# Summing each group's four edge tiles in one burst, and building one-hot matrices two groups ahead

## The chip, the core and the metric

The kernel runs on one core of a Trainium2 chip. The core has five engines with an instruction queue each: TensorE (PE in the profile; PEld is its weight load), VectorE (DVE), ScalarE (ACT), GpSimd (POOL) and SyncE (SP). Each takes its own queue in order and waits on semaphores for the others. The metric is the device time of one execution in microseconds; before the change its median was 3282.5 us over 3 runs.

## The reference

The input is a graph of 6250 nodes with 512 features each (f32) and 100,000 edges, sorted by their target. The output is

```python
x = x + gnn(layernorm(x), src, dst)      # two layers
x = x + moe(layernorm(x))                # 8 experts, the best 2 of each node
# one layer of gnn:
agg = segment_sum(h[src], dst)           # sum of the source rows of a node's edges
h = relu(h @ W_self + (agg / max(deg, 1)) @ W_neigh + b)
# moe, per expert: relu(x @ W1 + b1) @ W2 + b2, layernorm with gamma and beta,
# weighted by the softmax of the two best logits x @ Wg
```

## The kernel before

**Tiles.** The edges are cut into 782 tiles of 128. Three consecutive tiles make a chunk; its targets lie within 32 nodes from the chunk's first. Four chunks fill the 128 partitions of one PSUM tile `pa`, 32 partitions (a strip) each. The sum over edges is a matmul: a one-hot matrix of 128 edges x 32 nodes (`hot`) is the stationary operand, the 128 gathered source rows of 512 features are the moving one. A matmul in f32 is two instructions in the profile.

**Slots.** The loop `sums` (L194) runs over slots `i`. A slot is the four tiles, one of each chunk, with the same place in their chunks; three slots close a group of twelve tiles. There are 196 slots in a layer (the last has two tiles), and 49 blocks of 128 output nodes, about one per four slots. For each slot:

- `gather(i + ahead)` (L210) issues four indirect DMAs on GpSimd's queue (L214), each of 128 rows of 2 KB. They land in a ring: 16 buffers in stage 1 (`rows_t`, three slots ahead), 12 in stage 2 (parts of `big`, two ahead). A gather waits until the matmul that read its buffer last is done.
- `build(i + 1)` (L218) makes the next slot's one-hot matrices on VectorE (L224), in one of four buffers. In stage 1 it also adds the slots of a group up for the counts of edges (L234, `few`).
- `add` (L237) runs the four matmuls (L244), each on its own 32 columns of the array. The slot's work named "mid" stands between the second and the third of them.
- `close` (L247), at the end of a group, copies `pa` to a strip in SBUF on ScalarE (L252), and in stage 1 counts by a matmul (L256) and a copy (L259).
- The work named "post" comes last. `take_out` (L272) is one of it: it picks a block's 128 nodes from the strips by matmuls with `sel` (L278; L280 for the counts), made by `prepare` (L269).

**Stage 1** (`layer1`, L379) does the first GNN layer and the projections for the second. `take_out` starts a chain for each block: `u0` (post, one slot later) projects the block's own rows (L386). `u1` (mid, two later) transposes the aggregate (L188, four transpositions, copied from PSUM by ScalarE, L190), and `u2` (post, same slot) projects the copy (L386). `u3` (mid, three later) and `u4` (post, same slot) do the same with the result, `u5` follows a slot later.

**Stage 2** (`route`, L761) does the second aggregation, routes each node and fills experts' work in. Its chain is `turn` (mid, 2; L188 and L190), `logits` (post, 2; L775 and a copy L777), `experts` (mid, 3; L781, then VectorE), `rank` (mid, 4; L793, L794, then VectorE), two `send`s (mid, 5 and 6; an indirect DMA on GpSimd, L823), `turn_gates` (post, 5; L809) and `share` (post, 6; L816, L817). From about slot 77 on, every second slot starts an expert's tile: `turn_x` (mid; L188 and L190), `times` (post, same slot; L709, copied by L712) and `turn_h` (post, next slot; L717, L720).

The order on TensorE, VectorE, ScalarE and GpSimd is that of the program's text here (a manual schedule). Stage 3, after it, runs the rest of the experts and combines. `apart` (L533) writes one element on GpSimd (L535); before, only the sends of the last four blocks have it ahead of them.

Of the kernel before, what the change touches and what calls it, by code (L numbers as in the profile page):

```python
# [40 lines left out]
SW = 32  # L41
NQ = P // SW
TS = 3
# [24 lines left out]
def gnn_moe(ctx, tc, x, src, dst, Ws1, Wn1, gb1, Ws2, Wn2, gb2, Wg, W1, b1, W2, b2, gamma, beta, out):  # L68
    nc = tc.nc
# [7 lines left out]
    NB = (N + P - 1) // P  # L77
    rows = [min(P, N - b * P) for b in range(NB)]
    NT_E = (E + P - 1) // P
# [114 lines left out]
    def sums(z, pool, pap, room, pn, finish, ring, nring, each=None):  # L194

        nslot = (NG - 1) * TS + min(TS, NT_E - (NG - 1) * NQ * TS)  # L200
        ahead = nring // NQ - 1
        tiles = [[t for t in range(i // TS * NQ * TS + i % TS, min(NT_E, (i // TS + 1) * NQ * TS), TS)]
                 for i in range(nslot)]
        gathered, hots, few, strips, counts, sels, due = {}, {}, {}, {}, {}, {}, {}
        pa = [None]

        def at(i, place, what):
            due.setdefault((i, place), []).append(what)

        def gather(i):  # L210
            if i < nslot:
                for t in tiles[i]:
                    gathered[t] = ring()
                    nc.gpsimd.indirect_dma_start(  # L214
                        out=gathered[t], out_offset=None, in_=z[:, :],
                        in_offset=bass.IndirectOffsetOnAxis(ap=srcT[:, t : t + 1], axis=0))

        def build(i):  # L218
            if i >= nslot:
                return  # L220
            g, j = divmod(i, TS)
            m = len(tiles[i])
            hots[i] = pool.tile([P, NQ, SW], F32, name="hot", bufs=4)
            nc.vector.tensor_tensor(  # L224
                hots[i][:, :m],
                rel.rearrange("p (c j) -> p j c", j=TS)[:, j, g * NQ : g * NQ + m]
                .rearrange("p (t o) -> p t o", o=1).to_broadcast([P, m, SW]),
                iota_row[:, :SW].rearrange("p (o m) -> p o m", o=1).to_broadcast([P, m, SW]), OP.is_equal)
            if pn is not None and j:

                end = j == TS - 1 or i == nslot - 1
                few[g] = pool.tile([P, NQ, SW], BF16 if end else F32, name=f"few{int(end)}", bufs=1)
                before = hots[i - 1] if j == 1 else few[g, 1]
                nc.vector.tensor_add(few[g][:, :m], before[:, :m], hots[i][:, :m])  # L234
                few[g, j] = few[g]

        def add(i, qs):  # L237
            g, j = divmod(i, TS)
            if pa[0] is None:
                pa[0] = pap.tile([P, D], F32, name="pa", bufs=2)  # L240
            for q in qs:
                if q < len(tiles[i]):
                    t = tiles[i][q]
                    nc.tensor.matmul(pa[0][q * SW : (q + 1) * SW], hots[i][:, q], gathered.pop(t), start=(j == 0),  # L244
                                     stop=(j == TS - 1 or t == NT_E - 1), tile_position=(0, q * SW))

        def close(i):  # L247

            g = i // TS
            k = len(tiles[i]) * SW  # L250
            st = pool.tile([P, D], F32, name="st_", bufs=most)
            nc.scalar.copy(st[:k], pa[0][:k])  # L252
            strips[g] = st, k
            pa[0] = None
            if pn is not None:
                nc.tensor.matmul(pn[:k, 0], few[g].rearrange("p q m -> p (q m)")[:, :k], ones_h[:, :NDEG],  # L256
                                 start=True, stop=True)
                counts[g] = pool.tile([P, NDEG], F32, name="counts", bufs=most + 1)
                nc.vector.tensor_copy(counts[g][:k], pn[:k, 0])  # L259
            for b in range(NB):  # L260
                if reach[b][1] == g:
                    at(i + 1, "mid", lambda b=b: prepare(b))
                    at(i + 1, "post", lambda b=b: take_out(i + 1, b))

        def prepare(b):
            for g in range(reach[b][0], reach[b][1] + 1):
                k = strips[g][1]
                sels[b, g] = pool.tile([P, P], F32, name="sel", bufs=most)
                nc.vector.tensor_scalar(sels[b, g][:k], iota_row[:k], float(b * P), node[:k, g : g + 1],  # L269
                                        op0=OP.add, op1=OP.is_equal)  # L270

        def take_out(i, b):  # L272
            a, z = reach[b]
            ps = room()
            for g in range(a, z + 1):
                st, k = strips[g]
                sel = sels.pop((b, g))
                nc.tensor.matmul(ps, sel[:k], st[:k], start=(g == a), stop=(g == z))  # L278
                if pn is not None:
                    nc.tensor.matmul(pn[:, 1], sel[:k], counts[g][:k], start=(g == a), stop=(g == z))  # L280
            for behind, place, what in finish(b, ps) if pn is None else finish(b, ps, pn[:, 1]):
                at(i + behind, place, what)

        for i in range(ahead):
            gather(i)
        build(0)
        i = 0
        while i < nslot or any(k[0] >= i for k in due):
            gather(i + ahead)
            if each is not None:  # L290
                for behind, place, what in each(i):
                    at(i + behind, place, what)
            build(i + 1)
            if i < nslot:
                add(i, (0, 1))
            for what in due.pop((i, "mid"), ()):
                what()
            if i < nslot:
                add(i, (2, 3))
                if i % TS == TS - 1 or i == nslot - 1:  # L300
                    close(i)
            for what in due.pop((i, "post"), ()):
                what()
            i += 1
# [31 lines left out]
    with tc.tile_pool(name="l0", bufs=3, side="right") as pool, \  # L336
# [15 lines left out]
        for i, (b0, m) in enumerate(batch):  # L352
# [5 lines left out]
            for t in range(m):  # L358
                mv, rs = norm_stats(pool, xt[:n, t], n)
                nc.vector.tensor_scalar(xn[:n, t], xt[:n, t], mv[:n, 0:1], rs[:n], op0=OP.subtract, op1=OP.mult)  # L360
                b = b0 + t
# [13 lines left out]
    with tc.tile_pool(name="s1", bufs=2, side="right") as pool, \  # L375
# [55 lines left out]
        with tc.manual_schedule(engines=HAND):  # L431
            sums(xn_d, pool, pap, lambda: pap.tile([P, D], F32, name="ps"),
                 pap.tile([P, 2, NDEG], F32, name="pn"), layer1,
                 lambda: pool.tile([P, D], F32, name="rows_t", bufs=16), 16)
# [91 lines left out]
    def free_of(inst, group, keep=()):  # L526

        tc.declare_no_dep(inst.ins, group=group, reason="distinct rows", keep=keep)
        tc.add_to_no_dep_group(group, inst.ins)
# [3 lines left out]
    def apart():  # L533

        nc.gpsimd.memset(tick, 0.0)  # L535
# [200 lines left out]
    with tc.tile_pool(name="s2", bufs=2, side="right") as pool, \  # L736
# [11 lines left out]
        def ring():  # L748
            nring[0] += 1
            return part(NW + (nring[0] - 1) % 12)  # L750
# [10 lines left out]
        def route(b, pa):  # L761
# [4 lines left out]
            t = {}  # L766
# [51 lines left out]
                nc.sync.dma_start(accs[r], acc[:n])  # L818

            def send(k):  # L820
                if b >= NB - 4:
                    apart()
                inst = nc.gpsimd.indirect_dma_start(  # L823
                    out=xs[:, :], out_offset=bass.IndirectOffsetOnAxis(ap=slot[:n, b, k : k + 1], axis=0),
                    in_=t["xn"][:n], in_offset=None)
                free_of(inst, "xs")
# [20 lines left out]
        def each(i):  # L847

            at_slot[0] = i
            j = up_next[0]  # L850
            if i % 2 or j >= upto_n[-1]:
                return []
            c = max(c for c in range(len(n0)) if n0[c] <= j)
            if ready.get(c, 1 << 30) > i:
                return []
            up_next[0] += 1
            u = Up(j, pool, psp)
            u.fetch()
            return [(3, "mid", u.turn_x), (3, "post", u.times), (4, "post", u.turn_h)]

        fetch_own(0)
        with tc.manual_schedule(engines=HAND):
            sums(z2, pool, pap, lambda: psp.tile([P, D], F32, name="ph"), None, route, ring, 12, each)
# [4 lines left out]
    with tc.tile_pool(name="io", bufs=2, side="right") as io, \  # L868
# [114 lines left out]
        def finish(i, e, py, mv, rs):  # L983
            nc.vector.reciprocal(rs, rs)
            y = io.tile([P, D], F32, name="y")
            nc.vector.scalar_tensor_tensor(y, py, mv[:, 0:1], gmb[:, bass.ds(e * D, D)],  # L986
                                           op0=OP.subtract, op1=OP.mult)
            nc.scalar.activation(y, y, AF.Copy, scale=rs)
            nc.sync.dma_start(ys[i * P : (i + 1) * P, :], y)
# [208 lines left out]
```

## Time and profile before

| what | us |
|---|---|
| median of 3 runs (3280.7 to 3284.3) | 3282.5 |
| the profiled execution | 3665.7 |
| its span, first to last instruction | 3663.9 |
| mean granted TensorE clock in it | 0.903 |
| stage 1 (150 to 1440 us of the span) | 1290 |
| stage 2 (1508 to 2920) | 1412 |
| stage 3 (2920 to the end) | 744 |

The page of the profile gives each engine's busy time, then the span in 40 slices (a digit is the busy share in tenths; PEclk is the granted clock), the chain of work that ended last, and groups of equal instructions. Other views are used too: busy time in stretches (windows), the waits (who waited for whom: microseconds, times, longest), and the timeline. In a timeline, `[0.30 <-PE pa L244]` is idle time of the engine ahead of the instruction and what ended it; "issue" is time in which it waited for nothing that the profile shows.

### The profile page before, as it was taken

The page shows a single profiled execution, that of the slowest core. Times are in us where ns is not written, and L with a number is a line of the kernel's source. Part 1 is how long each engine was busy: PE and PEld are TensorE (multiplying, and loading weights), DVE is VectorE, ACT ScalarE, POOL GpSimd, SP SyncE. Part 2 cuts the span into 40 slices and gives each one's busy share as a digit, 9 for nine tenths or more (in the row PEclk, how much of TensorE's full clock was granted, in tenths as well). Part 3 has the DMA queues.
Part 4 walks back from the last instruction along what each step waited for, and adds up shares of the span by engine and source line. Part 5 has one row for each costly group of instructions (what it writes and reads, how often), then busy time and mean ns, then how long its engine had stood idle before and what let it go on. Part 6 is the DMA issues. An engine that isn't in the chain of part 4 may idle for free.

```text
span 3663.9 us, 33902 instructions
## 1 busy us (share of the span) xinstructions
PE 3038.6 (83%) x9794; PEld 1156.2 (32%) x9794; DVE 1131.4 (31%) x4001; ACT 659.3 (18%) x1188; POOL 1800.4 (49%) x1970
## 2 busy tenths in 40 slices
PE   7778888999999999466666888888888877999994
PEld 3223333333333333111111333333333333334442
DVE  5311111111111111132233333433343334443464
ACT  1211111111111111011111222222222211222221
POOL 0266555555555552466666555555555438000253
PEclk9889999999999999777777888898898988999997
DMA  6566666665666653666666766666677634441496
GB/s 241 183 186 203 199 195 200 192 185 177 185 188 176 178 171 103 239 200 208 199 204 200 214 214 215 209 217 213 214 228 218 189 105 155 135 132 61 156 308 233
DMA packets 269498, 698.76 MB, mean 191 GB/s; under 512 B 42448, under 2 KB 44090, under 8 KB 269148
## 3 DMA queue, kind: packets, MB, share of 16 engines
q0 software_dynamic: 142912, 463.42, 42.9%
q1 hardware_dynamic: 121372, 224.59, 17.9%
q10 hardware_dynamic: 5024, 8.50, 0.7%
q8 instruction: 85, 1.39, 0.2%
q14 instruction: 105, 0.86, 0.1%
HBM read 557.43 MB, written 139.71 MB: 190 GB/s over the span
## 4 chain that ended last, share of the span: by engine, by line
PE 70%; another core or an unknown queue 10%; DVE 7%; issue 6%; DMA 4%; ACT 2%; SPq 0%; DVEq 0%; POOL 0%; ACTq 0%; POOLq 0%
PE pm L386 17%; PE pa L244 15%; PE py L969 9%; PE ph L709 7%; PE ph L278 5%; PE pt L188 4%; PE ph L945 3%; PE ps L278 2%; PE ph L816 2%; PE pm L366 2%; DMA out<-acc 1%; PE small L775 1%; DMA xt<-in_x 1%; PE pt L717 1%
## 5 line engine op out<-in xcount | busy, mean ns | idle before, releaser
L214 POOL DMA_INDIRECT rows_t<-xn_d,srcT x782 | 742.1, 949 | 654.9 <-PE pa L244 262.9
L214 POOL DMA_INDIRECT big<-z,srcT x782 | 752.6, 962 | 609.3 <-issue 167.9
L244 PE MATMUL pa<-big,hot 128*32 128x512 f32 x1564 | 443.9, 684 | 107.5 <-DVE hot L224 63.0
L969 PE MATMUL py<-w,hT 128*128 x840 | 395.4, 614 | 40.4 <-DVE y L986 21.8
L244 PE MATMUL pa<-rows_t,hot 128*32 128x512 f32 x1564 | 348.5, 632 | 93.1 <-DVE hot L224 30.0
L386 PE MATMUL pm<-wn,tT 128*128 128x512 f32 x784 | 368.6, 613 | 22.0 <-ACT tT L190 21.7
L709 PE MATMUL ph<-big,xgT 128*128 x544 | 288.7, 680 | 68.7 <-ACT xgT L190 24.0
L905 POOL DMA_INDIRECT big<-ys,yrow x98 | 107.4, 1096 | 427.6 <-DMA ys<-y 331.3
L969 PEld LDWEIGHTS py<-w,hT 128*128 128x128 f32 x840 | 153.6, 193 | 219.3 <-issue 172.1
L386 PEld LDWEIGHTS pm<-wn,tT 128*128 128x128 f32 x784 | 144.9, 195 | 207.8 <-issue 163.7
L709 PEld LDWEIGHTS ph<-big,xgT 128*128 128x128 f32 x544 | 113.2, 219 | 230.5 <-issue 143.9
L386 PE MATMUL pm<-ws,tT 128*128 128x512 f32 x392 | 181.1, 605 | 0.0
L190 ACT ACTIVATE tT<-pt 128x512 f32<-128x512 f32 x117 | 69.0, 596 | 565.4 <-PE pt L188 408.7
L244 PEld LDWEIGHTS pa<-big,hot 128*32 128x32 f32 x1564 | 65.9, 114 | 247.9 <-issue 111.7
L945 PE MATMUL ph<-big,xgT 128*128 x296 | 136.9, 605 | 0.0
L823 POOL DMA_INDIRECT xs<-big,slot x98 | 98.8, 1008 | 71.6 <-DVE g L560 44.0
L419 DVE COPY deg<-pn 128x1 f32<-128x1 f32 x49 | 7.7, 158 | 408.4 <-PE pn L280 245.2
L720 DVE TENSOR_SCALAR hT<-pt,b1T 128x128 f32<-128x128 f32 x272 | 76.6, 344 | 166.4 <-PE pt L717 132.3
L976 DVE BATCH_NORM_STATS2 st<-py 128x6 f32<-128x512 f32 x105 | 73.2, 697 | 160.2 <-PE py L971 157.8
L244 PEld LDWEIGHTS pa<-rows_t,hot 128*32 128x32 f32 x1564 | 47.4, 110 | 233.5 <-issue 130.8
L416 DVE TENSOR_TENSOR s<-pm,bb 128x512 f32<-128x512 f32 x49 | 33.9, 691 | 272.0 <-PE pm L386 272.0
L224 DVE TENSOR_TENSOR hot<-rel,iota_row 128x128 f32<-128x128 bf16 (+1 forms) x394 | 106.0, 281 | 26.6 <-issue 12.4
(622 smaller groups left out, 3391.5 us busy)
## 6 DMA issues: line engine op xcount, KB each, us to landing
xg<-xs SPq DMA_DIRECT2D x105, 256.0 KB
ys<-y SPq DMA_DIRECT2D x105, 256.0 KB
hd<-hT SPq DMA_DIRECT2D x68, 256.0 KB
hT<-hd SPq DMA_DIRECT2D x68, 256.0 KB
rows_t<-xn_d,srcT POOLq DMA_INDIRECT x782
big<-z,srcT POOLq DMA_INDIRECT x782
xt<-in_x SPq DMA_DIRECT2D x12, 1024.0 KB
xn_d<-xn SPq DMA_DIRECT2D x12, 1024.0 KB
```

The source lines that it names most:

```text
L188: nc.tensor.transpose(pt[:, c, :n], t[:n, c * P : (c + 1) * P], ident[:n, :n])
L214: nc.gpsimd.indirect_dma_start(out=gathered[t], out_offset=None, in_=z[:, :], in_offset=bass.IndirectOffsetOnAxis(ap=srcT[:, t : t + 1], a ...
L224: nc.vector.tensor_tensor(hots[i][:, :m], rel.rearrange("p (c j) -> p j c", j=TS)[:, j, g * NQ : g * NQ + m] .rearrange("p (t o) -> p t o" ...
L244: nc.tensor.matmul(pa[0][q * SW : (q + 1) * SW], hots[i][:, q], gathered.pop(t), start=(j == 0), stop=(j == TS - 1 or t == NT_E - 1), tile ...
L278: nc.tensor.matmul(ps, sel[:k], st[:k], start=(g == a), stop=(g == z))
L386: nc.tensor.matmul(ph, tT[:, c], w[:, c], start=(start and c == 0), stop=(stop and c == C - 1))
L709: nc.tensor.matmul(ph, self.xT[:, c], w1[:, bass.ds(self.e * KD + c * D, D)], start=(c == 0), stop=(c == C - 1))
L720: nc.vector.tensor_scalar(hT[:, c], pt[:, c], b1T[:, bass.ds(self.e * HC + c, 1)], 0.0, op0=OP.add, op1=OP.max)
L823: inst = nc.gpsimd.indirect_dma_start(out=xs[:, :], out_offset=bass.IndirectOffsetOnAxis(ap=slot[:n, b, k : k + 1], axis=0), in_=t["xn"][: ...
L905: nc.gpsimd.indirect_dma_start(out=yk[:n], out_offset=None, in_=ys[: ready[0] * P, :], in_offset=bass.IndirectOffsetOnAxis(ap=yrow[:n, b, ...
L945: nc.tensor.matmul(ph, u.xT[:, c], w1[:, bass.ds(u.e * KD + c * D, D)], start=(c == 0), stop=(c == C - 1))
L969: nc.tensor.matmul(py, hT[:, c], w2[:, bass.ds(e * KD + c * D, D)], start=(c == 0), stop=False)
```

## The change

Three edits. `add` runs all four matmuls of a slot one after the other, and the slot's "mid" work follows them, ahead of `close` and "post". `build` is called two slots ahead, and twice before the loop. `apart` stands ahead of every send.

```diff
-        def add(i, qs):
+        def add(i):
             g, j = divmod(i, TS)
             if pa[0] is None:
                 pa[0] = pap.tile([P, D], F32, name="pa", bufs=2)
-            for q in qs:
-                if q < len(tiles[i]):
-                    t = tiles[i][q]
-                    nc.tensor.matmul(pa[0][q * SW : (q + 1) * SW], hots[i][:, q], gathered.pop(t), start=(j == 0),
-                                     stop=(j == TS - 1 or t == NT_E - 1), tile_position=(0, q * SW))
+            for q, t in enumerate(tiles[i]):
+                nc.tensor.matmul(pa[0][q * SW : (q + 1) * SW], hots[i][:, q], gathered.pop(t), start=(j == 0),
+                                 stop=(j == TS - 1 or t == NT_E - 1), tile_position=(0, q * SW))
...
         build(0)
+        build(1)
...
-            build(i + 1)
+            build(i + 2)
             if i < nslot:
-                add(i, (0, 1))
+                add(i)
             for what in due.pop((i, "mid"), ()):
                 what()
             if i < nslot:
-                add(i, (2, 3))
                 if i % TS == TS - 1 or i == nslot - 1:
                     close(i)
...
             def send(k):
-                if b >= NB - 4:
-                    apart()
+                apart()
                 inst = nc.gpsimd.indirect_dma_start(
```

## Prediction

> **What bounds the kernel now.** I read the page's head and slices first, then the busy time by stage (windows), then one stretch of the timeline. The page:
>
> ```profile
> span 3663.9 us, 33902 instructions
> PE 3038.6 (83%) x9794; PEld 1156.2 (32%) x9794; DVE 1131.4 (31%) x4001; ACT 659.3 (18%) x1188; POOL 1800.4 (49%) x1970
> PE   7778888999999999466666888888888877999994
> POOL 0266555555555552466666555555555438000253
> PEclk9889999999999999777777888898898988999997
> ```
>
> TensorE is busiest, but it has a gap (digit 4) and then a weaker stretch of 6s, at a granted clock of 0.7. The stages cut at these points (columns: length, then busy time of PE, PEld, DVE, ACT and POOL, then PEclk, DMA share, GB/s):
>
> ```profile
> 150.00:1440.00 1290.00, 1174.17 (x3956) 438.37 (x3956) 223.45 (x800) 153.83 (x253) 740.58 (x781) 0.95 0.63 185
> 1508.00:2031.00 523.00, 328.24 (x1064) 91.35 (x1064) 152.54 (x655) 86.86 (x150) 333.31 (x346) 0.75 0.69 212
> 2031.00:2920.00 889.00, 750.83 (x2601) 278.21 (x2602) 325.70 (x1381) 212.46 (x365) 502.13 (x523) 0.89 0.69 215
> ```
>
> Stage 1 (first line) is TensorE's: 91% busy. Stage 2 splits where expert work begins to fill it. Its early part (77 slots) has TensorE 63% busy. There GpSimd's gathers set a floor: one takes 0.95 us and the next starts 0.30 us later, so a slot of four costs 5.0 us, and a send 1.29 us. 77 x 5.0 + 34 x 1.29 = 429 us of the 523. The late part (118 slots) is TensorE's again, but its floor is near: 118 x 5.0 + 60 x 1.29 = 667 us of 889.
>
> How a split slot runs, stage 1, full clock (start, length, instruction; a matmul in f32 is two of the counted instructions):
>
> ```profile
> 706.75 1.05 PE L244 MATMUL pa<-rows_t,hot 128*32 128x512 f32 x4
> 707.74 0.66 PE L188 MATMUL pt<-ident,h 128*128 128x128 f32 x4
> 708.32 1.05 PE L244 MATMUL pa<-rows_t,hot 128*32 128x512 f32 x4
> 708.49 0.60 ACT L190 ACTIVATE tT<-pt 128x512 f32<-128x512 f32 x1 [5.22 <-PE pa L244]
> 709.30 3.70 PE L386 MATMUL pm<-wn,tT 128*128 128x512 f32 x8
> ...
> 716.08 1.06 PE L244 MATMUL pa<-rows_t,hot 128*32 128x512 f32 x8
> 717.07 3.70 PE L386 MATMUL pm<-ws,tT 128*128 128x512 f32 x8
> ```
>
> Half a burst holds TensorE from 706.75 to 707.74 and again from 708.32 to 709.30, 0.98 us each. A whole burst (716.08 to 717.07) costs 0.99. A second half is thus worth 0.98 us. But see what it covers: the copy of the transposition (L190) runs 708.49 to 709.09 under it, and L386, which needs that copy, starts at 709.30.
>
> **What the Trainium skill says.** "TensorE: Matmul & The Clock Gate", Part 3: Packing small matmuls, says that matmuls on different column strips run at the same time; the trace agrees, 1.06 us for four strips and 1.05 for two. "TensorEngine Tiling (Array Packing)", Key Properties, says that a change of tiling mode drains the engine; L386's eight show 0.44 us of streaming each, (3.70 - 0.59) / 7, so 0.98 against 2 x 0.44 leaves about 0.10 us for it. "TensorE: Matmul & The Clock Gate", Part 1, says that an idle window halves the clock. The trace shows 0.75 in early stage 2, but a stretch of stage 1 with a wait of over 1 us (238.1 to 245.7) kept 1.00, so waits of that size cost no clock here.
>
> **The profiled execution against the median.** It took 3665.7 us (span 3663.9); the median is 3282.5, 383 us less. In it there are moments where all engines resume together after waits of 3 to 11 us that end at an unknown queue, each followed by half clock. I judge that most of these are absent from the timed runs. So I price everything at full clock, without those waits, and subtract the same microseconds from both.
>
> **The change, part by part.** In the order of the built programs, 94 of stage 1's slots and 158 of stage 2's have TensorE work between the halves; after, none.
>
> *Bursts, stage 1.* In all 94 the middle is a transposition (L188 x4) and the next large work is the projection of its copy. The second half goes (0.98), but L386 cannot come before the copy: from L188's start 0.75 to the copy's, 0.60 for the copy, about 0.2 to L386, 1.55 us, against 709.30 - 707.74 = 1.56 before. Saved: 0.01 x 94, taken as 0. The stall stays, its cover is gone. Bounds: 0.1 us gained or 0.3 lost per slot, -10 to +28 us.
>
> *Bursts, early stage 2.* 34 middles are only experts or rank (L781, L793/L794), with nothing following that needs them at once: 34 x 0.98 = 33 us. 17 are turns, where logits (L775) wait for the copy: 3 us at most. All lies beside gathers. The floor admits little: I take 10, bounds 0 and 63 (with the waits below).
>
> *Bursts, late stage 2.* 30 middles without a transposition: 29 us. 20 with L188 directly ahead of L709: nothing. In the other 57, small work lies between transposition and use (L809 0.3, L717 0.43, L781 0.2, L816 0.9 us), and covers as much of the copy: by their counts about 30 us. Together 59 us.
>
> *Hot two groups ahead.* The same builds (L224, 0.28 us), one slot earlier on VectorE. TensorE's waits for it:
>
> ```profile
> PE pa L244 <- DVE hot L224: 11.3, 10, 1.1
> ...
> PE pa L244 <- DVE hot L224: 51.6, 16, 11.2
> ```
>
> (late, then early stage 2: us, times, longest.) The late ones are real: after a take-out L833, L834, L176, L178, L181 and L839 stand ahead of L224 on VectorE, and TensorE stood 1.14 us at 2111.35. These 10 us go: late stage 2 can lose 59 + 10 = 69. Early ones of the usual length are 1.7 us, some 16, 27 us, within the 63 above; longer ones fall in the unexplained moments. With hot early, the gathers' landing is late next. In stage 1 VectorE waits total 69 us over 14 times (the largest line is 30.0 in 4), but they follow quick slots (1.1, 5.5 and 4.6 us from 764.7 on) in which TensorE outruns 5 us of gathers: nothing taken. No new wait: of four buffers three are alive; L234's single buffer is freed by the count's matmul (L256), for which L259 already waited on VectorE.
>
> *What the burst queues behind itself.* The middle now stands behind tiles three and four, whose gathers are issued 1.25 us apart: it can start up to 2.5 us later, and with it ACT's copies and VectorE's routing. In early stage 2 TensorE has that slack. No gather, SP transfer or send moves against another.
>
> *The memset ahead of each send.* 90 more. One in place:
>
> ```profile
> 2889.12 0.94 POOL L214 DMA_INDIRECT big<-z,srcT  x1 [0.30 <-PE pa L244]
> 2890.06 0.09 POOL L535 MEMSET tick<- 1x1 f32 x1
> 2890.37 0.99 POOL L823 DMA_INDIRECT xs<-big,slot  x1 [0.22 <-issue]
> ```
>
> The send starts 0.31 us after the gather's end, against 0.30 without: 90 x 0.01 = 1 us on GpSimd; bounds 0 and 90 x 0.09 = 8.
>
> **Sum.** Late stage 2: 69 us of TensorE against a floor. The twelve late slots from 2096 to 2188 took 92 us; two at half clock (10.1 us each, 6.8 for the same work later on), one with a wait of 7.9 (16.1, else 7.0) and two with shorter ones (2.6 together) put right, 74 us remain, against 67.8 of GpSimd (48 x 1.25 + 6 x 1.29), 6.2 us of room, 61 us over 118 slots. Two engines this close get in each other's way: I take 40. 40 + 10 + 0 - 0 = 50 us. The profile: 3616; the median: 3282.5 - 50 = 3232.
>
> **Rivals.** *The floor is no floor* (unprofiled gathers quicker, or the hot waits also in timed runs): 69 + 63, about 132 us, 3150. For it: GpSimd waits for TensorE in early stage 2 too; against it: its 1.25 us spacing holds for long runs. *The copy comes late* (slower): 94 + 20 + 7 = 121 slots have the use directly behind the transposition. If ACT has another copy of 0.6 us ahead, each pays 0.6 beyond the 0.98: 73 us lost against 50 won, 3305. It decides from 50 / 121 = 0.41 us per slot. For it: projections waited for the copy in 10 places already (18.9 us); against: ACT had been idle 5.22 us ahead of the copy shown. *Gathers hide all of it*: stage 2 already runs at GpSimd's pace, 3280.
>
> **How the numbers follow.** A measurement tells 0.2%, 6.6 us, from no change. Forecast 0.54 (its own range 3205 to 3262), floor lifted 0.20, copy late 0.18, hidden 0.08. Faster 0.74, same 0.08, slower 0.18. The range 3160 to 3300 leaves out about half of each of the first two rivals, 0.10 and 0.09.
>
> **What would show it.** Right: runs of L244 of eight instructions only; stage 1's length unchanged within 15 us, with new waits of about 1 us of L386 for tT L190; no wait of L244 for hot of 1 to 2 us; late stage 2 some 40 us shorter at the same clock; memsets without delay of the sends. Wrong: stage 1 longer by 30 or more (copy late), early stage 2 shorter by 40 or more (no floor), or waits for hot that merely turned into waits for the gathers.

## The result, and the profile after

| | median us | lowest to highest | profiled execution |
|---|---|---|---|
| before | 3283.4 | 3280.7 to 3287.1 | 3665.7 |
| after | 3235.3 | 3223.4 to 3236.8 | 3223.4 |

The ratio after to before is 0.9845, with a 95% interval of 0.982 to 0.987: 48 us faster. The forecast was 3232. The profiled execution of before that the prediction was made from was an outlier, 380 us above the timed runs; from here on "before" is the kernel before profiled once more (`e0_before_again`, the first experiment; median 3282.3 us, profiled execution 3280.9). The profiled execution of after was the fastest of its four, 12 us below their median, and its stage lengths have to be read with that in mind.

The head of the page after:

```profile
span 3221.5 us, 33796 instructions
PE 2776.3 (86%) x9794; PEld 1103.7 (34%) x9794; DVE 1129.9 (35%) x4001; ACT 647.8 (20%) x1188; POOL 1809.4 (56%) x2060
PE   6799999999999999577777888888888779999994
PEclk9899999999999999798998999999999889999997
```

The gap between the stages is still there, and so is a weaker stretch behind it, at 7s. That it was 6s in the profile of the prediction is not undone by the change: the kernel before, profiled again, has 7s too.

```profile
PE   7799999999999999587777999999998679999994
```

GpSimd (POOL) has 90 instructions more, 2060: the 90 memsets.

The stages, cut in both kernels at the same instructions (stage 1; early stage 2, to the first expert's tile; late stage 2). Before again, then after (length, busy time of PE, PEld, DVE, ACT, POOL, then granted clock, DMA share, GB/s):

```profile
151.98:1299.11 1147.13, 1138.95 (x3942) 428.30 (x3942) 222.81 (x794) 153.48 (x252) 741.21 (x779) 1.00 0.69 208
1372.25:1803.45 431.20, 323.67 (x1039) 84.86 (x1031) 151.23 (x649) 83.84 (x145) 327.13 (x338) 0.90 0.79 249
1803.45:2531.86 728.41, 683.38 (x2627) 255.14 (x2627) 326.87 (x1382) 213.58 (x370) 510.24 (x532) 0.99 0.83 266
```

```profile
151.02:1285.07 1134.05, 1057.83 (x3942) 419.35 (x3942) 222.08 (x795) 148.36 (x252) 740.09 (x779) 1.00 0.71 210
1357.15:1780.44 423.29, 319.40 (x1031) 85.49 (x1025) 147.19 (x635) 82.35 (x143) 323.56 (x366) 0.89 0.81 251
1780.44:2472.93 692.49, 607.43 (x2638) 247.88 (x2633) 327.65 (x1396) 210.24 (x371) 519.65 (x593) 0.97 0.86 282
```

Stage 1 is 13 us shorter, early stage 2 8, late stage 2 36. In stage 1 TensorE's busy time fell by 81 us and the stage by 13: 68 us turned into idle time. In late stage 2 its busy time fell by 76 and the length by 36: 40 us turned into idle time. So the change saves TensorE a lot of work time, and much of that comes back as waiting. The three stages together are 57 us shorter, against 48 between the medians: some 9 us of the 57 belong to the one execution profiled and not to the change. The rest of this document asks which waiting, and what stands behind it.

In stage 1 the view of the waits has one large line (us in total, times, longest):

```profile
PE pm L384 <- ACT tT L190: 70.1, 94, 1.0
```

That is the projection waiting for the copy of the transposition, once in each of the 94 slots counted in the prediction. Three lines of the timeline show one:

```profile
680.14 0.66 PE L188 MATMUL pt<-ident,a 128*128 128x128 f32 x4
680.89 0.60 ACT L190 ACTIVATE tT<-pt 128x512 f32<-128x512 f32 x1 [4.94 <-PE pn L254]
681.54 3.70 PE L384 MATMUL pm<-wn,tT 128*128 128x512 f32 x8 [0.74 <-ACT tT L190]
```

The copy starts 0.75 us after the transposition's start, takes 0.60 and the projection follows 0.05 later: 1.40 us, of which TensorE stands 0.74.

Late stage 2, TensorE's waits, before and then after:

```profile
PE pa L244 <- DVE hot L224: 18.8, 13, 3.1
PE ph L709 <- ACT xgT L190: 13.5, 18, 0.8
PE pt L188 <- DVE hT L720: 11.7, 10, 2.2
PE ph L278 <- DVE sel L269: 1.0, 1, 1.0
```

```profile
PE ph L707 <- ACT xgT L190: 45.2, 36, 3.2
PE ph L276 <- DVE sel L267: 12.1, 11, 1.8
PE pt L188 <- ACT xgT L190: 8.5, 11, 1.0
PE small L807 <- DVE gates L560: 8.3, 10, 1.9
```

The waits for `hot` are gone, those for `hT` too. The expert's matmul (L709, now L707) waits 32 us more for its transposed input, `take_out` (L278, now L276) 11 us more for `sel`, and `turn_gates` (L807) has a new wait of 8 us for `gates`.

GpSimd's waits in the same stretch, before and then after. Its gathers start no sooner than 0.30 us after the last one's end, so only what is above 0.30 each is a wait:

```profile
POOL big L214 <- PE small L794: 39.4, 26, 3.5
POOL big L214 <- PE pa L244: 35.3, 82, 3.7
```

```profile
POOL big L214 <- PE pa L242: 13.4, 33, 2.4
POOL big L214 <- PE small L792: 6.5, 12, 2.1
```

Before: 39.4 + 35.3 - 108 x 0.30 = 42 us above it. After: 13.4 + 6.5 - 45 x 0.30 = 6 us. Without these waits GpSimd would need 728.4 - 42 = 686 us in the one and 692.5 - 6 = 686 in the other, the same time for the same gathers. In this execution of the changed kernel it has next to no slack left in late stage 2.

### The profile page after: what moved, and what is told of

Read it like the earlier page. It is cut to its first block, busy times and chain, and to the rows that moved or that the text cites. A ratio compares the mean times of both kernels' runs of the same rounds, so it can differ in the third digit from the quotient of the medians.

```text
span 3221.5 us, 33796 instructions
## 1 busy us (share of the span) xinstructions
PE 2776.3 (86%) x9794; PEld 1103.7 (34%) x9794; DVE 1129.9 (35%) x4001; ACT 647.8 (20%) x1188; POOL 1809.4 (56%) x2060
## 4 chain that ended last, share of the span: by engine, by line
PE 67%; DMA 15%; DVE 7%; issue 4%; ACT 3%; POOL 3%; SPq 0%; ACTq 0%; DVEq 0%; POOLq 0%
PE pm L384 20%; PE py L966 10%; PE pa L242 9%; DMA big<-z,srcT 7%; PE ph L707 7%; PE ps L276 4%; PE ph L276 4%; PE ph L942 3%; PE pt L188 3%; ACT tT L190 2%; PE pm L364 2%; DMA rows_t<-xn_d,srcT 1%; POOL big L214 1%; DMA out<-acc 1%; DMA xs<-big,slot 1%
## 5 line engine op out<-in xcount | busy, mean ns | idle before, releaser
L384 PE MATMUL pm<-wn,tT 128*128 128x512 f32 x784 | 362.5, 605 | 72.9 <-ACT tT L190 72.9
L242 PE MATMUL pa<-big,hot 128*32 128x512 f32 x1564 | 346.8, 636 | 63.2 <-DMA big<-z,srcT 61.7
L707 PE MATMUL ph<-big,xgT 128*128 x544 | 263.7, 630 | 51.9 <-ACT xgT L190 48.2
L242 PE MATMUL pa<-rows_t,hot 128*32 128x512 f32 x1564 | 240.4, 606 | 18.7 <-DMA rows_t<-xn_d,srcT 17.5
L384 PEld LDWEIGHTS pm<-wn,tT 128*128 128x128 f32 x784 | 140.9, 189 | 234.2 <-issue 141.1
L384 PE MATMUL pm<-ws,tT 128*128 128x512 f32 x392 | 181.1, 605 | 0.0
L707 PEld LDWEIGHTS ph<-big,xgT 128*128 128x128 f32 x544 | 102.1, 197 | 179.1 <-issue 111.3
L242 PEld LDWEIGHTS pa<-big,hot 128*32 128x32 f32 x1564 | 59.3, 111 | 257.6 <-DMA big<-z,srcT 169.3
L942 PE MATMUL ph<-big,xgT 128*128 x296 | 136.9, 605 | 0.0
L985 ACT ACTIVATE y<-y,rs 128x512 f32<-128x512 f32 x105 | 75.8, 722 | 166.4 <-DVE y L983 166.4
```

The costliest lines, as they stand in the source:

```text
L384: nc.tensor.matmul(ph, tT[:, c], w[:, c], start=(start and c == 0), stop=(stop and c == C - 1))
L707: nc.tensor.matmul(ph, self.xT[:, c], w1[:, bass.ds(self.e * KD + c * D, D)], start=(c == 0), stop=(c == C - 1))
L942: nc.tensor.matmul(ph, u.xT[:, c], w1[:, bass.ds(u.e * KD + c * D, D)], start=(c == 0), stop=(c == C - 1))
```

## The experiments

**The kernel before again, and each edit alone.** Four kernels on one chip: the kernel before unchanged (`e0_before_again`); the burst alone (`e1_burst`: `add` as in the change, `build(i + 1)` and the memsets as before); `hot` two ahead alone (`e2_ahead`); the memset ahead of every send alone (`e3_apart`).

```diff
 # e2_ahead, on the kernel before
         build(0)
+        build(1)
...
-            build(i + 1)
+            build(i + 2)
```

```diff
 # e3_apart, on the kernel before
-                if b >= NB - 4:
-                    apart()
+                apart()
```

> The kernel before, unchanged, profiled once more. Theory A (the stalls of several microseconds in the first profile of it are not of the kernel): the span is within 1% of 3283 us, waits of L244 for hot longer than 3 us are gone or few, stage 1 takes 1150 to 1230 us and late stage 2 740 to 790. Theory B (a profile lengthens this kernel): about 3660 us again, with the same stalls in the same slots.

> The burst alone: hot one group ahead and the memset only in the last four blocks, as before. Theory A (the gain is the second halves whose cover nobody needed, in stage 2): 30 to 45 us below the kernel before, about 3245 us, stage 1 unchanged. Theory B (the gain is hot's earlier start): within 15 us of the kernel before. Theory C (both needed, since with the burst TensorE reaches the next slot earlier and then meets hot): 10 to 30 us below.

> Hot two groups ahead alone, the halves still split. Theory A: 5 to 20 us below the kernel before, about 3270 us (the waits of 1 to 2 us of L244 for hot go). Theory B: 35 us or more below, about 3245. Theory C: within 10 us.

> The memset ahead of every send alone. All theories: 0 to 8 us longer, about 3284 us; if GpSimd's queue sets the pace of early stage 2 and the memset isn't hidden, the full 90 x 0.09 = 8 us.

| edit | median us | ratio to before (95%) | stage 1 | early stage 2 | late stage 2 (clock) |
|---|---|---|---|---|---|
| none | 3282.3 | 1.0008 (0.9998 to 1.0018) | 1147.1 | 431.2 | 728.4 (0.99) |
| burst | 3242.2 | 0.9885 (0.9866 to 0.9903) | 1134.4 | 429.0 | 711.0 (0.95) |
| two ahead | 3255.4 | 0.993 (0.9915 to 0.9945) | 1145.5 | 425.1 | 709.3 (1.00) |
| memset | 3280.8 | 1.0002 (0.9994 to 1.001) | 1146.1 | 432.6 | 731.5 (0.99) |
| all three | 3235.3 | 0.9845 (0.982 to 0.987) | 1134.0 | 423.3 | 692.5 (0.97) |

The ratios of the first four rows are to the kernel before on their chip (median 3280.1 us). What follows:

- The second profile of the kernel before has a span of 3279.0 us, so the long moments of the first, in which all engines resumed together, are not the kernel's. Its time of 3665.7 us lies within the 3648 to 3667 of another chip, met further down, on which the kernel before took that long in every run; whether it was that chip is not known. Stage 1 and late stage 2 are 3 and 12 us below the ranges expected of them.
- The memset costs nothing that can be measured.
- Stage 1's 13 us are the burst's. In late stage 2 of these profiled executions the two edits add up: 17 + 19 = 36. They divide differently from the forecast, which gave 59 us of TensorE to the burst there and 10 to `hot`.
- By the medians they do not add up: 38 + 25 = 63 us over the whole kernel, against the 48 of all three together. The profiled executions of the burst, of two ahead and of all three lie 9 us above, 5 below and 12 below their medians, so the lengths in late stage 2 are good to some 10 us, and a part of the sum that is lost when the edits meet can be hidden in them.
- Two expectations failed in part: the burst was to leave stage 1 unchanged, and two ahead, with 25 us, is above the 5 to 20 expected of it.
- The burst alone lowers the clock in late stage 2. The traces record half clock there for 70 us of the burst's 711, 10 of the 728 before and 38 of the 692 with all three edits (half of each is full-speed time lost: 35, 5 and 19 us). With `hot` built earlier as well, the burst costs less of it.

**The transposition ahead of the burst.** If the uncovered copy is what the burst lost, it can be had back without halving: let the transposition stand ahead of the four matmuls. `e4_pre` adds a place "pre" ahead of `add` and moves `u1`, `turn` and `turn_x` to it. `e5_pre_more` moves `u4` a slot later too, behind the next burst, and `prepare` (which makes `sel`) to "pre".

```diff
 # e4_pre, on the kernel after
             build(i + 2)
+            for what in due.pop((i, "pre"), ()):
+                what()
             if i < nslot:
                 add(i)
...
-  (2, "mid", u1), (2, "post", u2), (3, "mid", u3), (3, "post", u4)
+  (2, "pre", u1), (2, "post", u2), (3, "mid", u3), (3, "post", u4)   # turn and turn_x: "pre" too
 # e5_pre_more, on e4_pre
-  (3, "post", u4)
+  (4, "post", u4)
-                    at(i + 1, "mid", lambda b=b: prepare(b))
+                    at(i + 1, "pre", lambda b=b: prepare(b))
```

> The changed kernel with the transpositions u1, turn and turn_x moved ahead of the burst, so that the whole burst lies over ScalarE's copy. Theory A (the burst's uncovered copy is a loss: about 0.74 us in each of stage 1's 94 slots, 45 us of waits for xgT in late stage 2): stage 1 shorter than the changed kernel's 1134 us by 47 x 0.74 = 35, late stage 2 (692 us) by 25 to 45; together about 3170 us. Theory B (the loss only changes its place: the transposition waits for its input instead, or GpSimd's floor holds late stage 2): within 12 us of the changed kernel, 3225 to 3245.

> The kernel of e4 with two moves more: u4 one slot later than u3, and prepare (sel on VectorE) ahead of the middle. Theory A: 35 us more off stage 1 (47 slots x 0.74), 20 to 35 us off stage 2 (the waits of L276 for sel, 23 and 12 us in the changed kernel's early and late part); about 3110 us. Theory B: VectorE's or ScalarE's chain is late next, and less than 15 us come beyond e4.

`e4_pre` took 3186.5 us, 0.972 of before (0.9702 to 0.9739); `e5_pre_more` 3152.1, 0.9602 (0.9585 to 0.9619), the fastest of all that kept the whole computation. The stages of `e5_pre_more`:

```profile
151.53:1218.45 1066.92, 1053.67 (x3942) 423.20 (x3942) 221.62 (x795) 153.51 (x252) 740.47 (x779) 1.00 0.73 223
1713.06:2399.34 686.28, 611.88 (x2629) 250.87 (x2627) 326.00 (x1382) 210.24 (x368) 516.00 (x594) 0.97 0.87 284
```

Stage 1 fell from 1134 to 1098 with `u1` ahead and to 1067 with `u4` later: 67 us, against the 70.1 us of waits for the copy. TensorE's busy time there is that of the changed kernel within 5 us, so what went is the wait, and only the wait. In late stage 2 the same kind of move gave 4 us (`e4_pre`, 688.7) and 6 (686.3), where 25 us or more were expected of each. There the wait of the expert's matmul for `xgT` stayed at 40.0 us (45.2), in 18 places (36), one of them of 9.0 us. And the transposition moved ahead now waits for its own input, in both kernels:

```profile
PE pt L188 <- DVE big L838: 18.2, 11, 1.7
```

In the changed kernel that wait was 0.3 us, so a part of the waiting did change its place.

Either that is all that happens there, or GpSimd, with its 6 us of slack, ends the stretch whatever TensorE does. The next runs ask that.

**A load on GpSimd.** Three memsets of 128x160 more per slot of stage 2, ahead of its gathers, in the changed kernel (`e6_load_after`) and in the kernel before (`e7_load_before`).

```diff
             if i < nslot:
+                if pn is None:          # stage 2; once a slot
+                    for _ in range(3):
+                        nc.gpsimd.memset(extra, 0.0)
                 for t in tiles[i]:
```

> The changed kernel with three memsets of 128x160 on GpSimd ahead of each slot's gathers in stage 2, some 0.5 to 0.65 us a slot more on GpSimd's queue. Theory A (GpSimd sets the pace of early stage 2 and is no limit in late stage 2, where it has 692 - 667 = 25 us of room): early part longer by 40 to 50 us, late part by 35 to 50 (its new floor is 667 + 118 x 0.6 = 738); about 3325 us. Theory B (GpSimd's floor holds the late part too, the reason in the prediction): early 40 to 50, late the full 60 to 75; about 3350 us. If neither part is at the floor: less than 15 us early.

> The same load in the kernel before. Theory A: early part (431 us) longer by 30 to 45 us, late part (728 us, 60 us above its floor) by 10 to 25; about 3335 us. Theory B: late part longer by 40 us or more, about 3365 us.

They took 3413.6 us (1.0399 of before, 1.0379 to 1.042) and 3428.9 (1.0448, 1.0429 to 1.0467). The load was larger than expected: in the timeline of `e6_load_after` the three memsets take 0.84 us, and the next gather starts 0.46 us behind them in place of 0.30, 1.00 us a slot. Early stage 2 (77 slots) grew by 78 us in the changed kernel, 423.3 to 501.1, and by 72 in the kernel before, 431.2 to 502.8: GpSimd's queue is the bound there in both.

The early and the late stretch, changed kernel and then kernel before, each with the load:

```profile
1358.73:1859.85 501.12, 371.79 (x1031) 90.29 (x1023) 147.96 (x637) 82.18 (x144) 377.33 (x590) 0.88 0.68 211
1859.85:2665.11 805.26, 687.55 (x2634) 263.24 (x2635) 327.68 (x1394) 210.38 (x371) 602.18 (x949) 0.95 0.77 242
1370.36:1873.11 502.75, 377.02 (x1040) 91.36 (x1032) 150.92 (x650) 83.70 (x145) 375.61 (x559) 0.89 0.68 212
1873.11:2678.40 805.29, 732.53 (x2627) 264.80 (x2627) 327.57 (x1381) 213.41 (x370) 596.75 (x890) 0.97 0.76 242
```

The late stretch takes 805.3 us in both, though TensorE is busy 45 us less in the changed kernel. With the load GpSimd is the bound, and the change is worth nothing in that stretch. The number fits: GpSimd's 686 us without the load, and 118 slots by 1.00 us, are 804, for both kernels. The 25 us of room of theory A (692 - 667) would have made it 785. So without a load the bound stands at about 686, and `e5_pre_more` is at 686.3.

By the medians the load cost the changed kernel 178 us (3235.3 to 3413.6). With 78 of them in early stage 2, about 100 are left for the late part, 18 less than the load's 118. So in a usual execution of the changed kernel GpSimd's slack in late stage 2 is nearer 18 us than the 6 of the fast one profiled. This is an estimate; no other execution was profiled.

**Less for GpSimd.** The other direction: in stage 2 a slot gathers three tiles and uses the third one's rows for the fourth as well, in the kernel before (`e8_light_before`), the changed one (`e9_light_after`) and the one with the transpositions ahead (`e10_light_pre`).

```diff
-                for t in tiles[i]:
+                for q, t in enumerate(tiles[i]):
+                    if pn is None and q == 3:
+                        gathered[t] = gathered[tiles[i][2]]
+                        continue
                     gathered[t] = ring()
```

> The kernel before, but in stage 2 a slot gathers three of its four edge tiles and adds the third's rows twice; the fourth tile's rows are left out. GpSimd's work of a slot falls from 5.0 to 3.75 us, TensorE's stays. Only the comparison with the next run counts. Both theories: TensorE has 683 of the late stretch's 728 us and no wait for a gather there, so late stage 2 stays about 715 to 730; early stage 2 loses its 37 us of waits for gathers, 431 to about 395. Total about 3240.

> The changed kernel with the same three gathers in a stage 2 slot. Theory A (GpSimd's pace is what ended the gain at 36 us in late stage 2; its gathers there stand 6 us longer than their least, against 46 before): with the pace lifted the missing part comes out, late stage 2 some 65 to 70 us shorter than in the previous run (about 655), early stage 2 some 30 shorter, the sum with stage 1's 13 about 105 us less than the previous run. Theory B (TensorE's own waits for the copy xgT, sel and gates, and the clock that they cost, ended it): late stage 2 stays near 690, 36 less than the previous run, and the sum is about 55 us less.

> The version with the transpositions ahead of the burst, with the same three gathers in a stage 2 slot. With the full gathers it gained 67 us in stage 1 and only 6 in late stage 2 over the changed kernel. Theory A: GpSimd's pace also hid what the earlier transpositions give in late stage 2 (57 turns with a copy in the open, 0.3 to 0.7 us each): late stage 2 another 20 to 35 us below the previous run. Theory B: the transpositions only change places there, late stage 2 within 8 us of the previous run; the total is then 75 below it.

They took 3545.9, 3592.7 and 3443.9 us, 0.9693 (0.9661 to 0.9725), 0.982 (0.9798 to 0.9842) and 0.9402 (0.9387 to 0.9418) of a kernel before that took 3659.3 on the chip that they got. The traces have the waits of the first profile, in which several engines stand and resume together (at 342 us of `e8_light_before` VectorE, ScalarE and TensorE resume within 0.8 us of each other, after 9.7, 11.1 and 6.5 us). In stage 1, where the code of the first two differs from before and after in nothing, they took 1283 and 1315 us, against 1147 and 1134. The three runs don't answer what they were made for. They show one thing beside it: on this chip `e9_light_after`, with the change, was 47 us slower than `e8_light_before`, without it. Neither the change itself was run on it nor `e8_light_before` on another chip, so whether the chip alone turned the order round is not shown.

So the second of the three once more, on a chip on which the kernel before took 3280.1 us:

> The changed kernel with three gathers in a stage 2 slot once more (the fourth tile's rows are left out), since the chip of the last three runs took 3659 us for the kernel before and stalled all engines together. On a chip on which the kernel before takes about 3280: theory A (GpSimd's pace ended the gain in late stage 2) has late stage 2 at 650 to 670 where the changed kernel with all four gathers took 692, and the total near 3180. Theory B (TensorE's own waits and the clock they cost) has it at 685 to 695 and the total near 3200 to 3210, the rest of the difference being early stage 2, which loses its waits for gathers (58 us) under both.

3134.8 us, 0.9546 of before (0.9512 to 0.958). Early and late stage 2:

```profile
1359.25:1713.65 354.40, 265.60 (x1032) 77.98 (x1027) 146.11 (x635) 82.68 (x143) 253.73 (x293) 0.87 0.77 246
1713.65:2391.91 678.26, 598.37 (x2638) 246.58 (x2631) 327.46 (x1396) 210.05 (x371) 401.41 (x471) 0.97 0.74 240
```

Early stage 2 is 69 us shorter than in the changed kernel (423.3): the gathers were its bound. The gathers left out are worth 77 x 1.25 = 96 us there, so something else ends it at 354. Late stage 2 is 14 us shorter (692.5), between the two theories; the total is below what either expected. GpSimd is busy 401 of 678 us there and no longer near, and yet TensorE stands as long as before, 80 us in 85's place, its waits for `xgT` at 42.3. So in late stage 2 two bounds lie close together: GpSimd's at about 686 us, and TensorE's own path with its waits at 678. Taking away either one alone gives little; `e5_pre_more` is at the first, this run at the second. Both taken away together, `e10_light_pre`, was run on the chip of 3659 us only.

## Why the prediction was right, and where it was not

The total was right, 3232 against 3235, and so was the main idea, a gain in late stage 2 that GpSimd cuts short. That it agrees within 3 us is luck in part: the terms are 0, 10 and 40, the stages of the profile 13, 8 and 36, and 9 us of these are not in the medians. Its terms, in the order of its steps:

**The profiled execution against the median.** Right: the waits at which all engines resume together are neither in the timed runs nor in the second profile.

**Bursts, stage 1: forecast 0, measured -13.** The reading was right (the stall stays and its cover is gone: 94 waits of L384 for `tT`, 70.1 us, and the stage within 15 us). The mis-sized term is the step from the copy's end to the projection, put at about 0.2 us: it took 0.05. The 0.2 had been read from a line in which the half burst held TensorE until the projection's start (709.30), so it was not the copy that the projection had waited for. From the transposition's start to the projection is 1.40 us, not 1.55; 0.15 x 94 = 14 us.

**Early stage 2: forecast -10, measured -8.** Right, and for its reason, GpSimd's floor, though the floor's 429 us were too many: the stage took 423. Before, TensorE waited 64.0 us for `hot` and 36.7 for gathers in it. After, the waits for `hot` are 0.6 us and the gathers are late next:

```profile
PE pa L242 <- DMA big<-z,srcT: 58.2, 72, 4.4
PE ph L276 <- DVE sel L267: 23.3, 11, 2.6
```

Those for gathers grew by 22 us, those for `sel` by 17 (from 5.9), and so most of the 64 us only changed their name. The prediction has waits for `hot` that turn into waits for gathers among its signs of being wrong; here, where it had taken only 10 us, they agree with it. The runs with a load (78 and 72 us more) and `e11_light_again` (69 us less) show that the gathers set this stretch. "No floor", which needed 40 us or more here, is out. "Gathers hide all of it" holds for this stretch and not for the whole.

**Late stage 2: forecast -40 (69 of TensorE, cut by GpSimd's floor), measured -36.** The cut is real: GpSimd's waits fell from 42 to 6 us, and with a load on it both kernels took 805.3. The size is right in the execution profiled; by the estimate from the load it is some 12 us less in a usual one. The 40 itself was no sum but a guess below 61 us of room, and that room, read from twelve slots of the first profile, was 42 us in the second. Under it, two steps failed by which the burst gave less, and a third by which `hot` gave more; that they came out near 40 together is luck.

- "Waits of that size cost no clock here", said of waits of about 1 us, was read from a stretch of stage 1, and late stage 2 had been forecast at the same clock. In late stage 2 of the changed kernel it is wrong. The Trainium skill, "TensorE: Matmul & The Clock Gate", Part 1, has the clock halve after an idle window of about 3.4 us. Here much shorter waits were followed by half clock, 6 of the 24 waits of 0.7 to 1.2 us and 5 of the 24 longer ones, so that figure is no safe limit in this case. Two cases, each with the 3.4 us before and the 3.4 us after. In the first the wait is 3.2 us, for `xgT`, in the second 1.04 us, for `sel`:

```profile
2040.60:2044.00 3.40, 0.85 (x2) 0.49 (x3) 2.69 (x8) 0.78 (x2) 2.49 (x4) 1.00 0.94 286
2044.00:2047.40 3.40, 3.40 (x5) 1.35 (x4) 0.00 (x0) 0.00 (x0) 2.77 (x3) 0.50 0.97 343
2071.30:2074.70 3.40, 2.36 (x12) 1.07 (x9) 2.59 (x16) 2.50 (x3) 2.59 (x5) 1.00 0.81 231
2074.70:2078.10 3.40, 3.40 (x5) 1.35 (x4) 1.45 (x5) 0.00 (x0) 2.69 (x3) 0.50 0.91 314
```

  TensorE was busy for 2.36 of the 3.4 us before the second. Which waits are followed by half clock, and why in late stage 2 of the kernel before none of 37 waits of 0.7 to 1.2 us was, is not settled. The stretch lost 14 us of full-speed time more than before, and with the burst alone 30 more. The burst's forecast 59 us lacked 42 (17 measured), and this can be a large part of them; how much of it lengthened the stage is not shown.
- What stands behind the burst was examined in early stage 2 only. In late stage 2 VectorE's routing and `sel` come later too: waits for `sel` and `gates` grew from 1 to 20 us. The prediction had taken nothing for them.

On the other side `hot` was worth 19 us and not 10: its waits were 18.8 us in an undisturbed execution, 11.3 in the one read. And with GpSimd's floor lifted after the change the gain is 50 us (728.4 to 678.3) and not 69, so the 69 was too large and the floor's share smaller (14 us) than the 29 put down to it. This takes for granted that the kernel before would not gain from fewer gathers there; it had no waits of TensorE for gathers, but with three of four it was run on the chip of 3659 us only. The single losses named here overlap and are not settled to the microsecond.

**The rival "the copy comes late".** It did not decide, but half of its condition is there. Of the expert's waits for `xgT`, 18 are of 1.7 us or more. ScalarE's queue explains them:

```profile
2005.52 0.63 PE L188 MATMUL pt<-ident,xg 128*128 128x128 f32 x4
2007.02 0.29 ACT L180 ACTIVATE rs<-mv,eps 128x1 f32<-128x1 f32 x1 [4.86 <-DVE mv L178]
2007.22 0.58 ACT L190 ACTIVATE xgT<-pt 128x512 f32<-128x512 f32 x1
2007.86 1.55 PE L707 MATMUL ph<-big,xgT 128*128 x3 [1.70 <-ACT xgT L190]
```

The copy could start at about 2006.3, 0.75 us after the transposition's start as in stage 1. It stands behind L180, the square root of a block's layernorm, which waits for VectorE's L178 until 2007.0 while ScalarE is idle for 4.86 us. The kernel before had the same queue, with 0.73 us of waiting at the same place (18 times, 13.5 us), because the half burst of 0.98 us covered the rest: 0.73 + 0.98 = 1.71. So these 18 gained nothing, as forecast, but nothing was lost beyond it. In `e5_pre_more` the order of L180 and the copy is unchanged, and so is the wait (1.76 us at 2011.68). Its one wait of 9.0 us is of this kind too: L180 waited for L178 until 1975.72, and the copy came behind it at 1975.92. Giving the copy its place ahead of L180 was not tried.

**The memset.** Right: no delay that can be measured, a ratio of 1.0002 for the memset alone.

## What to carry to other kernels

A piece of work that splits a burst may be the cover of a copy: before joining the halves, put the transposition ahead of the whole burst, so that the join doesn't open the wait (48 us from the change as it was, 129 with the transpositions, `u4` and `prepare` moved as well). When the two busiest engines of a stretch are within a few per cent of each other, what one of them saves is worth at most the slack of the other (here 42 us, of which at most 36 came out). Read that slack from the idle time above an instruction's normal spacing, not from busy shares. Take such readings from an execution whose time is that of the timed runs.

## What the runs showed of the hardware

- A wait of TensorE of about 1 us in a busy stretch can be followed by 3.4 us at half clock (0.50 behind a wait of 1.04 us in the case shown); in late stage 2 of the changed kernel that came behind 6 of 24 waits of 0.7 to 1.2 us and 5 of 24 longer ones.
- A memset of 0.09 us between a gather and a send took none of GpSimd's time: the send started 0.30 us after the gather's end with it and without. Three memsets of 0.28 us did add their full time and 0.16 us more.
- The same kernel took 3280 to 3281 us on three chips and 3659 on another, in all seven timed runs there.
